# Cross-attention block: the Q, K, V and output products by seven blocks with sums in PSUM, softmax weights left undivided, and a new order on all engines

## The chip, the core and the metric

The kernel runs on one core of one Trainium2 chip. TensorE (PE) multiplies and writes only to PSUM; VectorE (DVE) and ScalarE (ACT) read and write PSUM and SBUF; GpSimd (POOL) works in SBUF; SyncE (SP) issues the transfers. The metric is the device time of one launch in microseconds (us). The median of the three runs is 1484.5 us (1484.43 to 1484.63).

## What is computed

There are 128 sequences of 128 tokens with 256 features, and a context of the same shape. All arithmetic is in fp32. Cut to what matters (16 heads of 16 features, `mask` is 0):

```python
q = (x @ Wq + bq) split into heads; k = (ctx @ Wk + bk); v = (ctx @ Wv + bv)
scores = q k^T / sqrt(16);  allowed = j < i;  scores = where(allowed, scores, -1e30)
attn = softmax(scores);  attn[:, :, 0, :] = 0
y = (attn v, heads joined) @ Wo + bo
x1 = layer_norm(x + y, ln1_g, ln1_b)
out = layer_norm(x1 + relu(x1 @ W1 + b1) @ W2 + b2, ln2_g, ln2_b)
```

W1 widens 256 to 1024 features and W2 brings them back.

## The kernel before

Two sequences make a pair, and one step handles one pair p: there are 64. The steps are a software pipeline. Step p computes the scores and the exponentials of pair p, the queries and keys of pair p+1, the weighted sum (`weigh`) and the output product of pair p-2, the W1 product of pair p-3 and the W2 product of pair p-4, and stores pair p-5. Pairs 0 to 6 fill the pipeline with code of their own, steps 7 to 62 are alike (`step`), step 63 and a written-out tail drain it. The order of the instructions on every engine is the order in which the functions are called: nothing reorders them, and an engine that waits holds up all that stands behind on it.

All of PSUM is one tile `banks` of eight banks of 512 columns. Scores of the high half of the rows take banks 0 to 3, of the low half banks 4 to 7, and the products take the same banks in turn.

**Products.** Q, K, V and the output product are each one block product of 256 x 256 weights with 256 columns: four matmuls of 128 x 128 weights by 256 columns (`project`, line 270; `values`, line 325; `attention_out`, line 573). In the trace every fp32 matmul is two records. The W1 and W2 products are already done by seven blocks (Strassen's scheme in Winograd's form): seven products of half blocks in place of eight, with sums of halves on the input side (`combine_normed`, `combine_hidden` on GpSimd) and sums of the products on the output side (`Hidden.u2` to `add5`, `sum_of_seven` on VectorE).

**Softmax.** ScalarE takes the exponential of each of the 32 head halves of a step, with the row sum beside it (`exponential_by_head`, line 839). VectorE takes reciprocals (`inverse`), GpSimd multiplies the weights by them in place (`divide`, line 485, three instructions a step), VectorE transposes 32 x 32 blocks into `tb` (`turn`, line 497), and 16 transfers a step move the blocks across partitions into `pT` (`bring`, line 512), from which `weigh` reads. The tiles `sm`, `tb` and `pT` share four buffers of one pool (`wide`).

**Norms.** Each of the two layer norms has its own statistics on VectorE and its own two scale factors on GpSimd (`deviation`, `shift`). ScalarE applies both (lines 625 and 662). The normed rows are transposed through DRAM (`turn_x1`): four transfers out, one back (lines 246 and 251).

**Transfers.** SP's queue holds in a step, in this order: 4 loads of x or of the context (line 92), in every second step one of the token rows (line 99), 4 plus 1 for the normed rows, the store (line 679), and the 16 of `bring`.

Of the kernel before, what the change touches and what calls it, by code (L numbers as in the profile page):

```python
# [10 lines left out]
ALU = mybir.AluOpType  # L11
# [8 lines left out]
def tile_cross_attention_block(  # L20
# [99 lines left out]
    def row(v, name):  # L120
        t = const.tile([P, v.shape[1]], F32, tag=name, name=name)
        nc.sync.dma_start(t, v.to_broadcast([P, v.shape[1]]))
        return t
# [11 lines left out]
    power = const.tile([P, 2, 1], F32, tag="power", name="power")  # L135
# [8 lines left out]
    table = const.tile([P, 2, 1], F32, tag="table", name="table")  # L144
# [3 lines left out]
    bo_r = row(bo, "bo_r")  # L148
# [7 lines left out]
    be1_r = row(ln1_b, "be1_r")  # L156
    b2_r = row(b2, "b2_r")
# [102 lines left out]
    def add_bo(p):  # L260
        st = states[p]
        st["xb"] = proj.tile([P, 2, D], F32, tag="xb", name=f"xb_{p}")
        nc.gpsimd.tensor_tensor(
            st["xb"], tokens_of[p // 2][:, p % 2 * 2 : p % 2 * 2 + 2], bov_r[:, None, :].to_broadcast([P, 2, D]), ALU.add
        )
# [92 lines left out]
    def wide(name):  # L358
        return soft.tile([P, NS * (H + HH) * 32], F32, tag="wide", name=name, bufs=4)

    def room(p, hi):

        st = states[p]
        if "sm" not in st:
            st["sm"] = wide(f"sm_{p}")
# [111 lines left out]
    def inverse(p, hi):  # L477
        st = states[p]
        rs = st["rs", hi] = small.tile([P, H], F32, tag=f"rs{hi}", name=f"rs{hi}_{p}")
        nc.vector.reciprocal(rs, st["su", hi])  # L480

    def divide(p, hi, part):
        st = states[p]
        sm = st["sm", hi]
        nc.gpsimd.tensor_tensor(  # L485
            sm[:, part, :], sm[:, part, :],
            st["rs", hi][:, part, None].to_broadcast([P, part.stop - part.start, sm.shape[2]]),
            ALU.mult,
        )
# [74 lines left out]
    def context(p):  # L564
        pc = states[p].pop("pc").rearrange("p (u i) -> p u i", i=P)
        nc.scalar.copy(cxT.rearrange("p m s i -> p (m s) i")[:, :, 1:], pc[:, :, 1:])  # L566
# [14 lines left out]
    def stats(p, t, i):  # L581
        st = states[p]
        mv = st["mv", i] = small.tile([P, 2, 2], F32, tag=f"mv{i}", name=f"mv{i}_{p}")
# [5 lines left out]
    def deviation(p, i):  # L589
# [3 lines left out]
        nc.gpsimd.tensor_scalar(ve, st["mv", i][:, :, 1:2], LN_EPS, None, ALU.add)  # L593
        nc.gpsimd.tensor_tensor(sd, ve, power, ALU.pow)

# [62 lines left out]
    def norm2(p):  # L658
        st = states[p]
        t2, sd, nb = st["t2"], st["sd", 2], st["nb", 2]  # L660
        for s in range(2):
            nc.scalar.activation(
                t2[:, s], t2[:, s], AF.Identity, bias=nb[:, s], scale=sd[:, s]
            )
# [74 lines left out]
    def turn_x1(p, queue=nc.sync, last=None, between=None):  # L739
        st = states[p]  # L740
        tb = ffn.tile([P, NS, 4 * 32], F32, tag="tbx", name=f"tbx_{p}")
# [25 lines left out]
    def hidden(p, fs, between=None, banks=(2, 3, 4, 0)):  # L767
        st = states[p]
        if fs[0] == 0:
            st["hT"] = ffn.tile([P, FC, TP], F32, tag="hT", name=f"hT_{p}", bufs=1)  # L770
# [60 lines left out]
    def exponential_by_head(p, hi, heads, summed=False):  # L831

        st = states[p]
        if summed and ("su", hi) not in st:
            st["su", hi] = small.tile([P, H], F32, tag=f"su{hi}", name=f"sa{hi}_{p}")
        sm, nmx = st["sm", hi], st["nmx", hi]
        for h in heads:
            src = st["sps", 1][h // 4][:, h % 4 * P : h % 4 * P + P] if hi else sm[:, h, :]
            nc.scalar.activation(sm[:, h, :], src, AF.Exp, bias=nmx[:, h : h + 1], scale=1.0, **(  # L839
                {"accum_out": st["su", hi][:, h : h + 1]} if summed else {}  # L840
            ))

    wt = const.tile([P, 4, FC // 2, P], F32, tag="wt", name="wt")
# [113 lines left out]
    class Hidden:  # L957
# [3 lines left out]
        def __init__(self, p, **where):  # L961
# [5 lines left out]
            else:  # L967
                self.hT = ffn.tile([P, FC, TP], F32, tag="hT", name=f"hT_{p}", bufs=1)
# [57 lines left out]
        def plain(self, fs, at):  # L1026
            ps = at_bank(at, f"ph_{self.p}_{fs[0]}")
            for i, f in enumerate(fs):
                self.plains[f] = ps[:, i * TP : (i + 1) * TP]
                for k in range(KC):  # L1030
# [4 lines left out]
                    )  # L1035

# [161 lines left out]
    def load_ahead(p):  # L1198
        if p % 2 == 0 and p + 4 < NP:
            load([p + 4, p + 5], "x")  # L1200
        if p % 2 == 1:
            if p + 3 < NP:
                load([p + 3, p + 4], "c")
            if 3 < p < NP - 1:
                load_tokens((p + 1) // 2)
# [106 lines left out]
    def fifth():  # L1312
# [34 lines left out]
        bring(p, nc.sync, LATE_FIRST)  # L1347
# [5 lines left out]
    def fall_in(p):  # L1353

        weigh(p - 2)
        context(p - 2)
        scores_both(p)
# [8 lines left out]
        exponential_by_head(p, 1, ONES)  # L1366
        mask_high(p, 2, 2)
        exponential_by_head(p, 1, TWOS)
# [3 lines left out]
        exponential_by_head(p, 0, ONES)  # L1372
        attention_out(p - 2)
        attention_sum(p - 2)
# [399 lines left out]
```

## Time and profile before

| | |
|---|---|
| median of three runs | 1484.5 us |
| span of the profiled execution | 1482.7 us |
| PE busy | 1475.0 us, 99% |
| DVE busy | 1386.3 us, 93% |
| ACT busy | 1324.1 us, 89% |
| POOL busy | 1376.5 us, 93% |
| transfers | 204.63 MB, mean 138 GB/s |

The page gives no time of the profiled execution beside its span; its span is 1.8 us below the median of the runs. Weighted sums of one step to the next start 22.63 us apart in each of the 56 steps 7 to 62, so these steps are 1267.6 us of the span; about 138 us lie ahead of them and 77 us behind. Matmuls are pipelined, so a busy PE tells only that there was always one in flight; how long a product holds PE is read from the starts of the product behind it.

### The profile page before, as it was taken

Reading aid. Unit: us, or ns where it says so; the run is one execution under the profiler, and the core shown is the slowest. Engines: PE = TensorE matmul, PEld = TensorE weight load, DVE = VectorE, ACT = ScalarE, POOL = GpSimd, SP = SyncE. Lnnn points to the kernel's source line nnn. Section 1 sums busy time; section 2 is a strip of 40 time slices with the busy share of each in tenths; the row PEclk is TensorE's granted clock in tenths of the full one; section 3 lists DMA queues with packets and bytes.
Section 4 is the critical chain, followed back from the end, with each engine's and each line's share of the span. In section 5 each row is a group of like instructions: output and inputs, shape, how many; then the busy total and the mean of one; then the engine's idle time right before and its main releaser. Section 6 shows DMA issues by size and latency. Waiting matters only on the chain.

```text
span 1482.7 us, 53916 instructions
## 1 busy us (share of the span) xinstructions
PE 1475.0 (99%) x19367; PEld 1378.1 (93%) x19367; DVE 1386.3 (93%) x2444; ACT 1324.1 (89%) x5272; POOL 1376.5 (93%) x1530
## 2 busy tenths in 40 slices
PE   9999999999999999999999999999999999999998
PEld 7788999999999999999999999999999999999998
DVE  7999999999999999999999999999999999999977
ACT  6668999999999999999999999999999999999963
POOL 6979999999999999999999999999999999999987
PEclk9999999999999999999999999999999999999999
DMA  8366666555655566665556556566655666555451
GB/s 201 79 133 150 148 150 141 127 146 138 154 144 133 138 146 138 149 144 130 144 132 156 146 128 143 144 137 150 145 132 141 136 153 148 128 141 131 109 137 51
DMA packets 415317, 204.63 MB, mean 138 GB/s; under 512 B 282448, under 2 KB 383056, under 8 KB 415056
## 3 DMA queue, kind: packets, MB, share of 16 engines
q1 hardware_dynamic: 412768, 199.34, 57.5%
q8 instruction: 160, 2.62, 0.8%
q10 hardware_dynamic: 2288, 1.85, 0.5%
q14 instruction: 101, 0.83, 0.2%
HBM read 70.26 MB, written 33.29 MB: 70 GB/s over the span
## 4 chain that ended last, share of the span: by engine, by line
PE 96%; DVE 2%; POOL 1%; ACT 0%; issue 0%; DMA 0%; POOLq 0%; DVEq 0%
PE banks L878 25%; PE banks L990 25%; PE banks L270 15%; PE banks L573 7%; PE banks L325 7%; PE banks L410 6%; PE banks L554 4%; PE banks L544 2%; PE banks L778 2%; PE banks L1042 0%; PE banks L797 0%; DVE su L468 0%; POOL sm L446 0%; PE banks L527 0%; POOL sm L470 0%
## 5 line engine op out<-in xcount | busy, mean ns | idle before, releaser
L839 ACT ACTIVATE sm<-banks,nmx 128x128 f32<-128x128 f32 x944 | 329.8, 377 | 16.3 <-DVE nmx L823 8.7
L485 POOL TENSOR_TENSOR sm<-sm,rs 128x1024 f32<-128x1024 f32 x171 | 322.6, 1901 | 0.0
L839 ACT ACTIVATE sm<-sm,nmx 128x64 f32<-128x64 f32 x944 | 312.5, 368 | 0.0
L497 DVE STREAM_TRANSPOSE tb<-sm 128x1024 f32<-128x1024 f32 x186 | 229.8, 1237 | 17.1 <-DMA pT<-tb 6.9
L1021 ACT ACTIVATE hT<-hT,b1e_c 128x256 f32<-128x256 f32 x464 | 198.1, 497 | 34.7 <-DVE hT L1009 21.0
L839 ACT ACTIVATION_READ_ACCUMULATOR sm<-sm,nmx 128x1 f32 x912 | 201.6, 221 | 0.0
L839 ACT ACTIVATION_READ_ACCUMULATOR sm<-banks,nmx 128x1 f32 x912 | 197.3, 216 | 0.0
L990 PE MATMUL banks<-xS,w1t 128*128 128x128 f32 x1392 | 174.4, 275 | 0.0
L878 PE MATMUL banks<-wt,hS 128*128 128x128 f32 x1440 | 170.7, 275 | 0.0
L878 PEld LDWEIGHTS banks<-wt,hS 128*128 128x128 f32 x1440 | 165.6, 192 | 0.1
L990 PEld LDWEIGHTS banks<-xS,w1t 128*128 128x128 f32 x1392 | 164.8, 192 | 0.0
L823 DVE TENSOR_REDUCE nmx<-banks 128x4 f32<-128x512 f32 x177 | 153.9, 869 | 6.0
L270 PE MATMUL banks<-xT,wq 128*128 128x256 f32 x504 | 125.4, 392 | 0.0
L315 ACT ACTIVATE kT<-banks,bkh,half 128x256 f32<-128x256 f32 x252 | 122.5, 590 | 2.8 <-PE banks L270 2.8
L990 PE MATMUL banks<-x1T,w 128*128 128x128 f32 x944 | 124.6, 275 | 0.2 <-DMA x1T<-x1t 0.2
L573 PE MATMUL banks<-wo,cxT 128*128 128x256 f32 x512 | 121.2, 379 | 0.0
L325 PE MATMUL banks<-wv,cT 128*128 128x256 f32 x512 | 121.0, 379 | 0.0
L270 PE MATMUL banks<-cT,wk 128*128 128x256 f32 x504 | 119.4, 380 | 0.1
L878 PEld LDWEIGHTS banks<-w,hT 128*128 128x128 f32 x944 | 114.7, 192 | 3.1
L990 PEld LDWEIGHTS banks<-x1T,w 128*128 128x128 f32 x944 | 114.9, 192 | 0.4 <-issue 0.3
L878 PE MATMUL banks<-w,hT 128*128 128x128 f32 x944 | 115.2, 275 | 0.0
L573 PEld LDWEIGHTS banks<-wo,cxT 128*128 128x128 f32 x512 | 97.0, 190 | 13.5 <-ACT cxT L566 0.3
(191 smaller groups left out, 3954.1 us busy)
## 6 DMA issues: line engine op xcount, KB each, us to landing
pT<-tb SPq DMA_DIRECT2D x976, 96.0 KB, 2.2
x1t<-tbx SPq DMA_DIRECT2D x252, 64.0 KB, 2.4
x1T<-x1t SPq DMA_DIRECT2D x63, 256.0 KB, 3.0
out_dram<-t SPq DMA_DIRECT2D x63, 256.0 KB, 3.1
xb<-in_x_dram SPq DMA_DIRECT2D x124, 128.0 KB, 3.7
cb<-in_ctx_dram SPq DMA_DIRECT2D x124, 128.0 KB, 4.2
x<-in_x_dram SPq DMA_DIRECT2D x31, 512.0 KB, 5.3
w<-in_L_xattn_W_dram SPq DMA_DIRECT2D x2, 1024.0 KB, 8.3
```

The source lines that it names most:

```text
L270: nc.tensor.matmul(ps[:, m * TP : (m + 1) * TP], w[:, k, m * P : (m + 1) * P], src[:, k, :], start=(k == 0), stop=(k == KC - 1),)
L315: nc.scalar.activation(st["kT"][:, m, e, :], pk[:, m * TP : (m + 1) * TP], AF.Identity, bias=bkh[:, m, e : e + 1], scale=half[:, e : e + 1],)
L325: nc.tensor.matmul(pv[:, s * D : (s + 1) * D], st["cT"][:, k, s * P : (s + 1) * P], wv[:, k, :], start=(k == 0), stop=(k == KC - 1),)
L410: nc.tensor.matmul(st["sps", hi][r][s * HP : (s + 1) * HP, m * 2 * n : (m + 1) * 2 * n].rearrange("p (e j) -> p e j", e=2), st["qT"][strip ...
L485: nc.gpsimd.tensor_tensor(sm[:, part, :], sm[:, part, :], st["rs", hi][:, part, None].to_broadcast([P, part.stop - part.start, sm.shape[2] ...
L497: nc.vector.transpose(st["tb"][:, :, at : at + 256].rearrange("p j (n a) -> p n j a", a=32), st["sm", hi].rearrange("p h j -> p (h j)")[:, ...
L573: nc.tensor.matmul(po[:, s * D : (s + 1) * D], cxT[:, k, s, :], wo[:, k, :], start=(k == 0), stop=(k == KC - 1),)
L823: nc.vector.tensor_reduce(st["nmx", 1][:, 4 * first : 4 * (first + n)], ps, AX.X, ALU.max, negate=True,)
L839: nc.scalar.activation(sm[:, h, :], src, AF.Exp, bias=nmx[:, h : h + 1], scale=1.0, **({"accum_out": st["su", hi][:, h : h + 1]} if summed ...
L878: nc.tensor.matmul(out, left(k), right(k), start=(k == 0), stop=(k == FC // 2 - 1))
L990: nc.tensor.matmul(ps[:, i * P : (i + 1) * P].rearrange("p (n a) -> p n a", a=32), left(i), right, start=True, stop=True,)
L1021: nc.scalar.activation(self.hT[:, f], self.plains.get(f, self.hT[:, f]), AF.Relu, bias=b1e_c[:, f : f + 1], scale=1.0,)
```

## The change

1. Q, K, V and the output product go by seven blocks too: seven matmuls of 128 x 128 by 128 columns in place of four by 256 columns. GpSimd forms the four sums of halves of each operand (`xc` of x, `cc` of the context for both K and V, `oc` of the attention context); the combined weights are formed once.
2. The sums of the products are made inside PSUM where the scheme allows it: a product block of class `Seven` is one bank with three regions a, b and f. Products 1, 6, 7 and 4 add onto a one after the other, 5 and 3 onto f, 2 goes to b. Between two of them ScalarE or VectorE takes the partial sum out of a, so PE must come back after that. W1 (`First`, three banks) and W2 (`Second`) now work in this way as well.
3. The exponentials stay undivided. All 32 row sums of a step go into one tile, VectorE takes the reciprocals and transposes them, SP writes them to DRAM (4 transfers) and reads them back broadcast (2 transfers), and `context` multiplies the attention context by them on VectorE in place of a ScalarE copy.
4. The two norms of a step share their statistics tiles and scale factors (`scales_of`); the second norm is applied on GpSimd (`norm2_on_pool`). `xb` is gone: the bias is added into the token tile in place. K is written once and spread to its two masked halves from SBUF (`spread`). The read back of the normed rows is issued a step later than the writes.
5. `sm`, `tb` and `pT` have one buffer each.
6. A step is a list of some 150 names, and each engine takes its own in the list's order. Names with -1 are run for the pair before. Pairs 7 to 62 use it.

```diff
@@ room, wide @@
-        return soft.tile([P, NS * (H + HH) * 32], F32, tag="wide", name=name, bufs=4)
+        return soft.tile([P, NS * (H + HH) * 32], F32, tag=name[:2], name=name, bufs=1)
@@ inverse and divide @@
-    def divide(p, hi, part):
-        st = states[p]
-        sm = st["sm", hi]
-        nc.gpsimd.tensor_tensor(
...
+    def inverse(p):
...
+        nc.vector.reciprocal(rs, st.pop("su"))
+        nc.vector.transpose(rt, rs)
+
+    def send_inverse(p):
...
+        for b in range(NS):
+            nc.sync.dma_start(mid[:, b], rt[32 * b : 32 * b + 32])
+
+    def fetch_inverse(p):
...
+        for m in range(KC):
+            nc.sync.dma_start(
+                inv[:, m].rearrange("p l s q -> p (l s q)"),
+                mid[m][:, None, :].to_broadcast([HH, DK, TP]),
+            )
@@ context @@
+            for l in range(2):
+                at = slice(l * HP + 1 - l, l * HP + HP)
+                nc.vector.tensor_tensor(
+                    cxT[:, :, :, at], pc[:, :, :, at], inv[:, :, l, :, 1 - l :], ALU.mult
+                )
@@ class Seven @@
+            for n in which:
+                out = self.of({2: 1, 5: 2, 3: 2}.get(n, 0))
...
+                for k in range(self.depth):
+                    nc.tensor.matmul(
...
+                        start=(n == 1 and k == 0), stop=(k == self.depth - 1),
...
+    class Queries(Seven):
...
+        def keep(self):
+            self.put(0, 0, self.a)
+            self.put(1, 1, self.f)
...
+        def keep2(self):
+            self.put(1, 0, self.a)
...
+        def add(self):
+            nc.vector.scalar_tensor_tensor(
+                self.q[:, 1, P:], self.a, QSCALE, self.q[:, 1, P:], ALU.mult, ALU.add
+            )
...
+        def rest(self):
+            self.put(0, 1, self.a)
@@ class Keys @@
+        def spread(self):
+            for e in range(2):
+                nc.scalar.activation(
+                    self.kT[:, :, e, :], self.k, AF.Identity, bias=0.0, scale=half[:, e : e + 1]
+                )
@@ the order of a step @@
+        weigh re2-1 inverse-1 res0-1 vr-1 tokc-1 re3-1 re0-1 hf-1 context scores res1-1 br3
...
+        load-1 hk ob w6 oa el3 xc3-1 stats2 xs0 kk q2 tokx xs1 el4 o4 cc3 sendi-1 w3 qk2 or
```

The first place is SP's queue. `inv` are the reciprocals in DRAM, `invb` their broadcast copy, `x1t` the normed rows in DRAM, `x1T` what is read back. Before, from one step's `pT` to the next:

```order
L512 DMA pT_12894<-tb_12765 32x768 x16
L92 DMA cb_13009<-in_ctx_dram 32x32x32 x4
L99 DMA x_13014<-in_x_dram 128x4x256
L246 DMA x1t_13222<-tbx_13219 32x4x128 x4
L251 DMA x1T_13221<-x1t_13222 128x4x128
L679 DMA out_dram<-t_32_12817 128x2x256
```

Now, from one step's first `pT` to its store (the token rows, `x`, come in every second step):

```order
L524 DMA pT_13454<-tb_13259 32x768 x4
L1918 DMA x1T_13476<-x1t_13328 128x4x128
L524 DMA pT_13454<-tb_13259 32x768 x12
L92 DMA xb_13570<-in_x_dram 32x32x32 x4
L490 DMA inv_13601<-rt_13405 32x32 x4
L498 DMA invb_13670<-inv_13601 128x1x256 x2
L99 DMA x_13686<-in_x_dram 128x4x256
L1913 DMA x1t_13701<-tbx_13688 32x4x128 x4
L730 DMA out_dram<-t_31_12748 128x2x256
```

Six transfers came in. The read back of `x1t` moved behind the next step's first four `pT`, and the read back of `inv` stands right behind its four writes.

The second place is PE behind the scores. Before, the four products of a step stand there in one piece (`wq`, `wo`, `wk`, `wv` are the weights, `w_139` is W2):

```order
L410 MATMUL banks<-kT_7739,qT_7719 64x128 x8
L270 MATMUL banks<-xT_7763,wq 128x256 x4
L573 MATMUL banks<-wo,cxT 128x256 x4
L270 MATMUL banks<-cT_7765,wk 128x256 x4
L325 MATMUL banks<-wv,cT_7410 128x256 x4
```

Now the blocks of V, of the output product, of Q and of W2 stand between each other (`wvt`, `wot`, `wqt`, `wt` are combined weights; `cc`, `oc`, `xc`, `hS` the combined halves):

```order
L409 MATMUL banks<-kT_7987,qT_7928 64x128 x8
L1146 MATMUL banks<-wv,cT_7832 128x128 x2
L1146 MATMUL banks<-wvt,cc_7968 128x128
L1146 MATMUL banks<-wo,cxT 128x128 x2
L1146 MATMUL banks<-wot,oc_8255 128x128
L1146 MATMUL banks<-w_138,hT 128x128 x4
L1146 MATMUL banks<-wvt,cc_7968 128x128
L1146 MATMUL banks<-wv,cc_7968 128x128
L1146 MATMUL banks<-xT_8015,wq 128x128 x2
```

PE no longer finishes a product before it starts the next: each product is cut into four parts, with other products between them.

The third place is ScalarE at the end of the exponentials. Before, the 32 exponentials (`sm<-`) are one piece, and the copies of Q, K, the hidden layer and V follow:

```order
L839 ACTIVATE sm_6556,sa_19_6614<-banks,nmx_19_6558 128x128 x16
L839 ACTIVATE sm_6556,sa_19_6635<-sm_6556,nmx_19_6557 128x64 x16
L296 ACTIVATE qT_6652<-banks,bqs_c 128x256 x2
L315 ACTIVATE kT_6672<-banks,bkh,half 128x256 x4
L999 COPY hT_6781<-banks 128x4x128
```

Now, up to the last block of Q (`kr` is K before it is spread, `x_32` the first norm):

```order
L891 ACTIVATE sm_12303,su_12384<-sm_12303,nmx_34_12304 128x64 x4
L668 ACTIVATE x_32_12552<-t_32_12363,nb_12525,sd_12524 128x256 x2
L1371 COPY hT<-banks 128x4x128
L891 ACTIVATE sm_12303,su_12384<-sm_12303,nmx_34_12304 128x64 x2
L1212 ACTIVATE kr_12450<-banks,bk_c 128x128
L891 ACTIVATE sm_12303,su_12384<-sm_12303,nmx_34_12304 128x64 x2
L1235 ACTIVATE kT_12451<-kr_12450,half 128x2x256 x2
L1174 ACTIVATE qT_12392<-banks,bqs_c 128x128
```

The exponentials are cut into groups of two to six heads, with the copies of partial sums between the groups.

More of the change, by code (lines that the diff above doesn't have):

```diff
@@ new lines, in residual1_one, with turn_x1_blocks @@
+    def residual1_one(p, n):
+        st = states[p]
+        if n == 0:
+            st["x1b"] = ffn.tile([P, 2, D], F32, tag="x1b", name=f"x1b_{p}", bufs=3)
+        nc.gpsimd.tensor_tensor(
+            st["x1b"], st["x1b"] if n else st["x1"],
+            (be1b_r if n else g1_r)[:, None, :].to_broadcast([P, 2, D]), ALU.add if n else ALU.mult,
+        )
+    def turn_x1_blocks(p):
+        st = states[p]
+        tb = st["tbx"] = ffn.tile([P, NS, 4 * 32], F32, tag="tbx", name=f"tbx_{p}", bufs=1)
+        nc.vector.transpose(
+            tb.rearrange("p j (u a) -> p u j a", a=32),
+            st["x1"].rearrange("p s (k j a) -> p (s k) j a", k=KC, a=32),
+        )
@@ L1560, in tile_cross_attention_block @@
     sixth(6)
-    for p in range(7, NP):
+    late = max(int((key + "-0").split("-")[1]) for key in ORDER)
+    for p in range(FIRST, NP - 1 + late):
         step(p)
+    last_step(NP - 1)
     VECTOR_ALONE = (nc.vector, nc.vector)
```

662 lines of the change are left out of this document (529 added, 133 removed).

## The prediction

> **What bounds the kernel now.** I read the page first, then a table of stretches, each one step long, then the timelines of the engines in one such step.
>
> The page, engine by engine, and the chain that ended last:
>
> ```profile
> span 1482.7 us, 53916 instructions
> PE 1475.0 (99%) x19367; PEld 1378.1 (93%) x19367; DVE 1386.3 (93%) x2444; ACT 1324.1 (89%) x5272; POOL 1376.5 (93%) x1530
> PE 96%; DVE 2%; POOL 1%; ACT 0%; issue 0%; DMA 0%; POOLq 0%; DVEq 0%
> ```
>
> One step, busy time of PE, weight loads, DVE, ACT, POOL, then the clock and the transfers:
>
> ```profile
> 313.13:335.76 22.63, 22.63 (x306) 21.36 (x306) 21.36 (x39) 21.34 (x90) 21.43 (x25) 1.00 0.58 129
> ```
>
> A step takes 22.63 us, PE never idles in it at clock 1.00, and the three other engines are at 94 to 95%. PE sets the pace, but whoever speeds up PE alone by 5% meets three other engines. There are 56 such steps, so 0.1 us a step is 5.6 us of the whole.
>
> PE's timeline in one step, from the Q product on (start, length, what):
>
> ```profile
> 344.97 1.99 PE L270 MATMUL banks<-xT,wq 128*128 128x256 f32 x8
> 346.80 1.89 PE L573 MATMUL banks<-wo,cxT 128*128 128x256 f32 x8
> 348.53 1.89 PE L270 MATMUL banks<-cT,wk 128*128 128x256 f32 x8
> 350.25 1.89 PE L325 MATMUL banks<-wv,cT 128*128 128x256 f32 x8
> 351.98 1.95 PE L878 MATMUL banks<-w,hT 128*128 128x128 f32 x16
> 353.77 1.06 PE L878 MATMUL banks<-wt,hT 128*128 128x128 f32 x8
> ```
>
> Starts tell the cost. The four products hold PE from 344.97 to 351.98, 7.01 us. Sixteen records of 128 columns take 1.79 us (351.98 to 353.77), so one takes 0.112.
>
> **PE after.** Each of the four products becomes seven matmuls, 14 records of 0.112: 1.57 us, 6.26 for all four. Everything else on PE keeps its count. The step falls by 0.75 to 21.88 us, if nobody keeps PE waiting.
>
> **ScalarE after.** Its timeline in the same step:
>
> ```profile
> 335.22 1.94 ACT L315 ACTIVATE kT<-banks,bkh,half 128x256 f32<-128x256 f32 x4
> 337.02 0.61 ACT L999 COPY hT<-banks 128x512 f32<-128x512 f32 x1
> 337.49 0.68 ACT L340 COPY vz<-banks 128x256 f32<-128x256 f32 x2
> 339.84 1.08 ACT L662 ACTIVATE t<-t,nb,sd 128x256 f32<-128x256 f32 x2
> 341.29 1.71 ACT L1021 ACTIVATE hT<-hT,b1e_c 128x256 f32<-128x256 f32 x4 [0.37 <-DVE hT L1009]
> 343.56 0.58 ACT L566 COPY cxT<-banks 128x508 f32<-128x508 f32 x1 [0.56 <-PE banks L554]
> 346.17 0.37 ACT L839 ACTIVATE sm<-banks,nmx 128x128 f32<-128x128 f32 x1
> 346.43 0.19 ACT L839 ACTIVATION_READ_ACCUMULATOR sm<-banks,nmx 128x1 f32 x1
> 357.13 0.85 ACT L296 ACTIVATE qT<-banks,bqs_c 128x256 f32<-128x256 f32 x2
> ```
>
> An activation of 128 columns holds ScalarE for 0.26 us (346.17 to 346.43); the two of Q now take about 0.72. Q becomes four of 128 columns, 1.04: plus 0.3. K costs 1.80 now (335.22 to 337.02); it becomes four of 128 columns, 1.04, and two spreads of 512, which I put at 0.65 each (the 512-column copy holds 0.47, plus what K's own 0.45 a piece shows of its pointer operands): plus 0.55. V's two copies become four: plus 0.3. The hidden copy becomes three: plus 0.95. The second norm and the context copy leave: about 1.0 and 0.45 less. The first half of the relus now reads PSUM: about 0.2 less. The net is 0.45 more. ScalarE is 21.34 busy with its ends counted, some 20.9 from start to start; after, 21.4, bounds 21.0 to 22.2.
>
> **VectorE after.** The prices by size, and the tail's rows for 128 columns:
>
> ```profile
> L919 DVE TENSOR_TENSOR t<-t,banks 128x256 f32<-128x256 f32 x120 | 50.6, 421 | 7.3 <-PE banks L878 3.3
> L1005 DVE TENSOR_TENSOR hT<-hT,banks 128x512 f32<-128x512 f32 x58 | 39.9, 688 | 7.0
> L1016 DVE TENSOR_TENSOR hT<-hT,banks 128x1024 f32<-128x1024 f32 x58 | 68.6, 1184 | 0.3 <-PE banks L990 0.2
> 1476.37 0.28 DVE L1706 TENSOR_TENSOR t_last<-banks,x1b 128x128 f32<-128x128 f32 x1
> ```
>
> Out go the sum of the output product (512 columns), five sums of W2 (512, twice 384, twice 256), six of the hidden layer (five of 512, one of 1024) and a reciprocal, together about 8.1 us. In come eleven adds of 128 columns (3.1), eight of 256, the two context products among them (3.4), three of 512 (2.1), the small transpose and the finer masks (0.5): 9.1. That is 1.0 more in durations; about 0.05 of each overlaps its neighbour (the step's 39 durations add up to some 23.2, busy is 21.4), so eleven more instructions give 0.5 back. VectorE comes to 21.8, bounds 21.2 to 22.4.
>
> **GpSimd after.** Its groups:
>
> ```profile
> L485 POOL TENSOR_TENSOR sm<-sm,rs 128x1024 f32<-128x1024 f32 x171 | 322.6, 1901 | 0.0
> L953 POOL TENSOR_TENSOR xS<-x1T 128x128 f32<-128x128 f32 x58 | 26.6, 458 | 0.0
> L594 POOL TENSOR_TENSOR sd<-ve,power 128x2 f32<-128x2 f32 x127 | 90.4, 712 | 10.6
> L1712 POOL TENSOR_TENSOR sd_last<-sd_last,power 128x1 f32<-128x1 f32 x2 | 1.3, 666 | 2.4 <-DVE sd_last L1711 2.4
> L593 POOL TENSOR_SCALAR ve<-mv 128x2 f32<-128x2 f32 x127 | 29.0, 228 | 15.2 <-DVE mv L587 4.7
> L1196 POOL TENSOR_TENSOR be1b_r<-be_r,b_r 128x256 f32<-128x256 f32 x1 | 0.7, 731 | 0.0
> ```
>
> Three divisions go: 5.7. Two sets of scale factors become one of four columns; the power costs 0.05 a column by the rows of one and two, so about 0.8, and the set about 1.3 less. Twelve sums of 128 columns come, 5.4. The second norm, two scalings of 256 columns, has no row: between 0.23 (two columns) and 0.73 (two inputs of 256 columns) each; I take 0.6, nearer to the row of its size. Sum: 0.4 less. Now 21.43 busy, 22.3 from start to start; after about 21.8 to 22.0, bounds 21.1 to 22.4. The Trainium skill, GPSIMD Engine Reference, section 3.1, puts a good loop at about 1.8 cycles an element where two inputs need 2.5. By that a scaling would be about 0.6, an estimate from that page, and GpSimd 21.9; no run here shows it.
>
> **SP's queue after.** SP computes nothing, but issuing takes its time, and a wait there holds up every later transfer. One step, and the waits of the queue (line waited for: total us, times, longest):
>
> ```profile
> 335.28 3.00 SPq L92 DMA_DIRECT2D cb<-in_ctx_dram  x4
> 338.32 1.98 SPq L99 DMA_DIRECT2D x<-in_x_dram  x1
> 340.71 1.84 SPq L246 DMA_DIRECT2D x1t<-tbx  x4
> 345.37 0.38 SPq L251 DMA_DIRECT2D x1T<-x1t  x1
> 345.85 0.45 SPq L679 DMA_DIRECT2D out_dram<-t  x1
> 346.38 10.99 SPq L512 DMA_DIRECT2D pT<-tb  x16
> SPq L251 <- DMA x1t<-tbx: 149.3, 109, 3.3
> ```
>
> Issuing takes 18.6 us in this step and 16.7 in one without token rows: 17.65 on average. On top SP stands from 342.55 to 345.37, 2.8 us, for the write to DRAM to land; over the 63 pairs 2.4 each. The change moves that read a step later, so the wait goes. It adds the same pattern anew: four small writes, with the read right behind them. The writes cost 1.2 (0.30 each, the shortest of `x1t`) to 1.84, I take 1.6; the two reads 0.38 to 0.45 each, 0.85; the landing 1.7 (the shortest `x1t`) to 2.8, I take 2.0, since fewer bytes go. Sum: 22.1, bounds 21.3 to 23.2. What used to hide it was 2 us of slack; the new step has less than none.
>
> **A deadline that is new.** `tb` had spare buffers and now has one. VectorE may write the next `tb` only when all 16 `pT` have landed:
>
> ```profile
> DVE tb L497 <- DMA pT<-tb: 6.9, 26, 1.4
> pT<-tb SPq DMA_DIRECT2D x976, 96.0 KB, 2.2
> ```
>
> The 16 can start only when `weigh` has read the single `pT`, about 1.5 us into the step. With 11.0 of issue, 0.4 of the read between them and 2.2 to land, the last is there at 15.1. VectorE reaches its `turn` by the sums above at about 13.9 to 14.5. It waits up to 1 us, and what stands behind on VectorE, about 9 us of work and at its end the context and the masks of the next step, comes late by as much. ScalarE has about 0.4 us to absorb that.
>
> **The sum.** PE 21.88, ScalarE 21.4, VectorE 21.8, GpSimd 21.9, SP 22.1; the largest is SP, and the deadline on `tb` pulls at the same figure. I add 0.15 for hand-overs, which were none before but are now four for each of six products, and take 22.25: 0.38 less in each of 56 steps, 21.3 us. Head and tail: the head loses six GpSimd divisions or their like and gains 24 small sums, the tail loses three and gains one trip through DRAM (about 5 us by the 2.4 and 3.0 us to land of `x1t` and `x1T`), so 0 to plus 5; I take plus 1. The span becomes 1482.7 - 21.3 + 1 = 1462.4, and the median, 1.8 above, 1464.
>
> **The rivals.**
>
> PE stays the bound (0.20): the handoffs fit, the landing is short, pT's issues come nearer to 0.6 each. Then 0.75 times 56: 42 off, 1443. For it speaks that PE lost nothing before with three engines at 95%.
>
> An engine's own work becomes the bound (0.10): VectorE or GpSimd at their upper 22.4 give 13 off, 1472.
>
> SP's queue makes it slower (0.22). Mechanism: SP waits for the four writes of the reciprocals as long as it waits for `x1t` today, with the upper issue costs: 17.65 + 1.84 + 0.9 + 2.8 = 23.2. It decides from 22.63 on, that is from 2.2 us of landing with these issue costs. Then 0.57 times 56 more: 1516. For it: the writes stand right behind four loads, as `x1t` stood behind the token rows when it took 2.8. Against it: they are far smaller.
>
> No change (0.04): SP at 22.6.
>
> The seven blocks save nothing (0.04). TensorE loads weights for every matmul, 56 loads in place of 32 for the four products, and the weight loads:
>
> ```profile
> L878 PEld LDWEIGHTS banks<-wt,hS 128*128 128x128 f32 x1440 | 165.6, 192 | 0.1
> L325 PEld LDWEIGHTS banks<-wv,cT 128*128 128x128 f32 x512 | 97.1, 190 | 13.2
> ```
>
> If a load that follows a wait is not hidden, 24 more at 0.19 are 4.6 us and the step grows by up to 3.9; already 0.75 undoes the gain. At half of that, 1.2 net, the time is 1552. The rows speak against it: in the existing seven blocks a load has 0.115 of busy time and the matmul behind it comes at 0.112, waits included. The Trainium skill, TensorE: Matmul & The Clock Gate, section LDWEIGHTS, gives 128 columns / 1.2, 107 ns, and Perfetto Trace Analysis, section Identifying the Most-Contended Engine, judges PE by its load share. By these the new blocks are bound by their loads; the trace's 0.112 agrees, and the sum already holds it.
>
> **How the numbers follow.** My forecast has 0.40. Faster: 0.40 + 0.20 + 0.10 = 0.70. Within 0.2%, about what a measurement of this kernel can tell: 0.04. Slower: 0.22 + 0.04 = 0.26. The range reaches from PE's bound, 1441, into the SP case as far as a step of 22.97, 19 us more: 1503. What lies beyond is most of the loads' case and half of SP's.
>
> **What would show it.** Starts of the weighted sums 22.25 apart; PE busy near 98% with idle time in front of the scores or `weigh`; SP's wait for `inv` near 2 us a step; VectorE waiting in `turn` for `pT`; records of 128 columns still 0.112 apart. The prediction is wrong if the step is below 21.9 or above 22.6, or if SP stands idle for over 2 us a step.

## The result, and the profile after

| | before | after |
|---|---|---|
| median of the runs | 1484.5 us | 1591.3 us (1584.8 to 1599.9) |
| ratio, 95% interval | | 1.072, 1.069 to 1.076 |
| span of the profiled execution | 1482.7 us | 1597.8 us |
| mean step, 7 to 62 | 22.63 us, all alike | 24.58 us, between 22.8 and 32.0 |

The change makes the kernel 7.2% slower; 1464 was forecast, with a range up to 1503. Of the 115 us more in the span, 56 steps with 1.95 more each make 109; the end after the last of them takes 4.0 more and the start 1.9. The longest step is the first in the new order (32.0). The profiled execution took 1599.9 us, the most of the six, so its steps stand some 0.15 us above those of the median.

First the busy time of the engines and the chain that ended last, by engine, from the page of the changed kernel.

```profile
PE 1508.3 (94%) x20711; PEld 1423.7 (89%) x20711; DVE 1328.2 (83%) x3114; ACT 1337.8 (84%) x5613; POOL 1398.5 (88%) x1933
PE 33%; SPq 29%; POOL 11%; DMA 9%; DVE 8%; issue 8%; ACT 2%; DVEq 0%; POOLq 0%; ACTq 0%
```

TensorE was busy 99% of the span and is at 94%; no engine is full. SP's queue, which computes nothing, has 29% of the chain. One step of that queue (start, duration, line, transfer, count):

```profile
707.40 3.34 SPq L524 DMA_DIRECT2D pT<-tb  x4
710.84 0.53 SPq L1918 DMA_DIRECT2D x1T<-x1t  x1
711.41 8.99 SPq L524 DMA_DIRECT2D pT<-tb  x12
720.45 2.86 SPq L92 DMA_DIRECT2D cb<-in_ctx_dram  x4
723.40 3.61 SPq L490 DMA_DIRECT2D inv<-rt  x4
728.17 1.31 SPq L498 DMA_DIRECT2D invb<-inv  x2
729.58 1.85 SPq L1913 DMA_DIRECT2D x1t<-tbx  x4
731.49 0.44 SPq L730 DMA_DIRECT2D out_dram<-t  x1
732.03 1.32 SPq L524 DMA_DIRECT2D pT<-tb  x1
```

From 707.40 to 732.03 SP issues or waits without a pause: 24.6 us. Its one long gap is from 727.01 to 728.17, where the reads of the inverses stand behind the landing of the four writes. With 23.5 us of issuing this is one of the long steps. Over all 56, with every pause of over 0.15 us between two issues counted as a wait, issuing takes 21.7 us a step (17.6 before), the pause ahead of the reads 1.7, and waits for engines and other transfers 1.2. The waits (line waited for: total us, times, longest) and two groups of GpSimd:

```profile
SPq L498 <- DMA inv<-rt: 85.7, 71, 2.9
DVE tb L509 <- DMA pT<-tb: 41.2, 26, 6.2
PE banks L1146 <- DVE t L1290: 30.0, 26, 5.2
PE banks L409 <- issue: 28.9, 19, 3.1
L713 POOL TENSOR_SCALAR t<-t,mv,sd 128x256 f32<-128x256 f32 x112 | 136.9, 1229 | 0.0
L1884 POOL TENSOR_TENSOR sd<-ve,power 128x4 f32<-128x4 f32 x56 | 58.1, 1038 | 0.0
```

Four causes could be read from these: SP's wait, the single `tb` (VectorE waits for `pT`, TensorE for the sums behind that), GpSimd, whose norm costs 1.23 us a half, and standstills of TensorE in the scores with no releaser. Each has 0.5 to 1.5 us a step, so the profile alone does not say which one sets it.

### The profile page after: what moved, and what is told of

Same layout as the page of the kernel before. It is cut to its first block, busy times and chain, and to the rows that moved or that the text cites. A ratio compares the mean times of both kernels' runs of the same rounds, so it can differ in the third digit from the quotient of the medians.

```text
span 1597.8 us, 56966 instructions
## 1 busy us (share of the span) xinstructions
PE 1508.3 (94%) x20711; PEld 1423.7 (89%) x20711; DVE 1328.2 (83%) x3114; ACT 1337.8 (84%) x5613; POOL 1398.5 (88%) x1933
## 3 DMA queue, kind: packets, MB, share of 16 engines
q8 instruction: 166, 2.72, 0.8%
## 4 chain that ended last, share of the span: by engine, by line
PE 33%; SPq 29%; POOL 11%; DMA 9%; DVE 8%; issue 8%; ACT 2%; DVEq 0%; POOLq 0%; ACTq 0%
SPq L524 24%; PE banks L1146 14%; PE banks L1355 10%; DMA pT<-tb 4%; DMA x<-in_x_dram 3%; PE banks L409 2%; PE banks L566 2%; DVE tb L509 2%; POOL t L713 2%; POOL x1b L1895 2%; SPq L1918 1%; PE banks L556 1%; DVE t L1290 1%; SPq L92 1%; POOL t L727 1%
## 5 line engine op out<-in xcount | busy, mean ns | idle before, releaser
L891 ACT ACTIVATE sm<-sm,nmx 128x64 f32<-128x64 f32 x944 | 320.5, 356 | 0.0
L409 PE MATMUL banks<-kT,qT 32*64 32x256 f32 (+1 forms) x3840 | 124.0, 336 | 34.1 <-issue 28.9
L1850 DVE TENSOR_REDUCE nmx<-banks 128x4 f32<-128x512 f32 x224 | 143.2, 681 | 0.0
L1839 POOL TENSOR_TENSOR hS<-hT 128x512 f32<-128x512 f32 x112 | 140.3, 1274 | 0.0
L409 PEld LDWEIGHTS banks<-kT,qT 32*64 32x64 f32 x3840 | 89.2, 132 | 57.1 <-issue 33.2
L713 POOL TENSOR_SCALAR t<-t,mv,sd 128x256 f32<-128x256 f32 x112 | 136.9, 1229 | 0.0
L1384 ACT ACTIVATE hT<-hT,b1e_c 128x256 f32<-128x256 f32 x224 | 95.6, 497 | 29.4 <-DVE hT L1380 29.4
L1290 DVE TENSOR_TENSOR t<-banks,t 128x256 f32<-128x256 f32 x224 | 69.0, 348 | 46.5 <-PE banks L1146 46.5
L1844 DVE TENSOR_TENSOR banks<-banks,neg 128x256 f32<-128x256 f32 x224 | 94.7, 423 | 4.5 <-PE banks L409 4.5
L1390 ACT ACTIVATE hT<-banks,b1e_c 128x256 f32<-128x256 f32 x224 | 94.5, 481 | 0.5 <-PE banks L1355 0.5
```

Source lines behind the costliest of these rows:

```text
L409: nc.tensor.matmul(st["sps", hi][r][s * HP : (s + 1) * HP, m * 2 * n : (m + 1) * 2 * n].rearrange("p (e j) -> p e j", e=2), st["qT"][strip ...
L713: nc.gpsimd.tensor_scalar(t2[:, s], t2[:, s], mv[:, s, 0:1], sd[:, s], ALU.subtract, ALU.mult)
L1384: nc.scalar.activation(self.hT[:, f, at], self.hT[:, f, at] if src is None else src, AF.Relu, bias=b1e_c[:, f : f + 1], scale=1.0,)
L1390: nc.scalar.activation(self.hT[:, 2 * i].rearrange("p (s t) -> p s t", s=2), banks[:, self.at : self.at + 2, i * P : (i + 1) * P], AF.Relu ...
L1839: nc.gpsimd.tensor_tensor(c[:, n], left, right, how)
L1844: nc.vector.tensor_tensor(ps[:, :, HP:], ps[:, :, HP:], neg[:, 1, None, :].to_broadcast([P, 4, HP]), ALU.add)
```

## The experiments

All are edits of the changed kernel unless another is named. Times are medians; before was 1484 us in every comparison. "Step" is the mean from start to start of `weigh` in the profiled execution, and the median step stands beside it where the two differ in meaning.

**SP and GpSimd: four kernels.** The second norm back on ScalarE; the inverses read later; both; the norm and no trip at all (that kernel multiplies the context by a constant, so it leaves the division out).

```
-        "norm2": lambda p: norm2_on_pool(p - 5),
+        "norm2": lambda p: norm2(p - 5),                      # e1, e3, e4
-  ... norm1 fetchi ka ...   h3 finish1 qr store-1 re1
+  ... norm1 ka ...          h3 finish1 qr fetchi store-1 re1  # e2, e3
-        "sendi": lambda p: send_inverse(p),
+        "sendi": lambda p: states[p].pop("rt"),               # e4
```

> The changed kernel with the second norm back on ScalarE, as before the change: two scalings of 1.23 us leave GpSimd (23.4 us of own work a step become 20.9), two of some 0.5 us come to ScalarE. If GpSimd's own work sets the step of 24.58, the step falls to the next bound, 22.3 to 23.0: 1465 to 1505 us. If SP's queue with the single tb and pT sets it, GpSimd only gets idle time: 1580 to 1600 us. If TensorE's standstills in the scores (28.9 us in all, no releaser shown) are a cost of their own, they stay in every kernel.

> The changed kernel with the read of the inverses moved in the order from ahead of the token rows to ahead of the store, after the writes of x1: same transfers, but SP no longer stands 1.6 us a step for the four small writes to land. If SP's queue sets the step: 24.58 less 1.6, 23.0, times 56: about 1500 us. If GpSimd's own work of 23.4 sets it: 1530 at the least (24.58 to 23.4 only if that idle time came from SP), or no change, 1580 to 1600.

> Both edits: second norm on ScalarE and the inverses read late. If SP alone sets the step: as the late read alone, about 1500. If GpSimd alone: as the norm alone. If both bind by turns, each alone brings little and the two together bring the step to 22.3 to 22.6: 1465 to 1485 us.

> Second norm on ScalarE, and the inverses' trip through DRAM left out in steps 7 to 62 (reciprocals are still computed; the context is multiplied by a constant, so the division is not done): 6 transfers and the wait for their landing go from SP, some 5 us a step. If SP's queue sets the step, TensorE's 21.9 to 22.1 becomes the bound: 1445 to 1460 us. If the step stays above 23 here, neither SP nor GpSimd's norm is the cause, and it is in the order of the work or TensorE's standstills: above 1500 us.

Measured: 1598.4, 1583.2, 1597.0 and 1547.9 us (steps 24.54, 24.32, 24.49, 23.75). GpSimd with 2.5 us less a step gains nothing, so alone it does not set the step here. The late read misses its forecast of 1500: SP's wait for the inverses is gone (1.4 us in all), but SP now stands for VectorE's transposed rows ahead of the writes of `x1t`, and the answer comes late.

```profile
SPq L1913 <- DVE tbx L1903: 96.2, 51, 5.7
DVE cxT L582 <- DMA invb<-inv: 74.9, 41, 3.8
PE banks L409 <- DVE cxT L582: 48.9, 44, 3.2
```

In that kernel the context waits for `invb`, and the scores for the context: part of the wait went from SP to TensorE. Without the trip 50 us go against the same norm on its own. That speaks for the trip, by SP's load or by its answer; but 1445 to 1460 was forecast for SP as the only bound, and the step stays at 23.75, so SP is not all.

**TensorE's code blocks and the sums behind `tb`: four kernels.** 23 times after step 7 starts, TensorE stood still over 0.2 us before an instruction that waits for nothing, 31.3 us in all, mostly in the scores; before, never. One such place, as a table of stretches (us, busy time and count of each engine, granted clock, DMA share, GB/s), and the instruction queue in the page:

```profile
316.00:318.00 2.00, 2.00 (x134) 1.82 (x124) 1.31 (x3) 1.52 (x5) 1.92 (x2) 1.00 0.82 210
318.00:320.00 2.00, 0.35 (x15) 0.00 (x0) 1.38 (x5) 1.75 (x5) 1.15 (x3) 1.00 1.07 336
320.00:322.00 2.00, 0.86 (x26) 0.59 (x26) 0.36 (x2) 0.00 (x0) 2.00 (x4) 1.00 0.31 103
322.00:324.00 2.00, 2.00 (x12) 2.00 (x13) 1.89 (x4) 0.96 (x5) 2.00 (x4) 0.62 0.45 110
324.00:326.00 2.00, 2.00 (x12) 2.00 (x11) 2.00 (x5) 0.94 (x6) 1.23 (x2) 0.53 0.70 219
326.00:328.00 2.00, 2.00 (x20) 2.00 (x20) 1.64 (x3) 1.52 (x8) 0.00 (x0) 1.00 0.66 160
q8 instruction: 166, 2.72, 0.8%
```

TensorE stands from 318.4 to 321.1, at first while the transfers fill every DMA engine. Soon after it runs 3.4 us at half its clock, which the rows of two us average to 0.62 and 0.53:

```profile
322.47:325.88 3.41, 3.41 (x19) 3.41 (x18) 3.41 (x8) 1.90 (x10) 2.76 (x3) 0.50 0.63 179
```

Counted through the trace (matmuls, weight loads, semaphore and empty instructions), all 23 standstills fall on the same number modulo 256, and at each of them TensorE goes on 1.2 to 1.6 us after a packet of the instruction queue has landed. The row `q8 instruction` has 2.72 MB in 166 packets, 16 KB each; TensorE's 42,670 instructions in 166 blocks are 257 a block. Before has 640 instructions a step, two and a half blocks, so the block's edge falls on the same two places for ever. 22 of the 640 are empty instructions in the second layer, and the new order has none:

```profile
L219 PEldq NOP  x1700: 13/13/13, 1.1 to 1468.6; - x189
L221 PEldq NOP  x468: 13/13/13, 1.1 to 1583.8; - x156
```

The first row is before's, the second after's; the difference is 22 in each of 56 steps. After has 668 instructions a step, and the edge wanders through the dense stretch of `weigh` and scores.

```
-  ... means k2 turn1 eh1 ... wb xs2 wa addbo turn0 el1 k3 w4 norm1 fetchi ka xc0 kb ...
+  ... means k2 eh1 ... wb xs2 wa addbo el1 k3 w4 norm1 fetchi ka turn1 turn0 xc0 kb ...   # e5, e7
+        fill()    # behind each matmul: empty ones, 36 in step 7, then 100 a step           # e6, e7
-                empty(after // (FC // 2) + (after % (FC // 2) > k))                         # e8, in before
```

> The changed kernel with one move in VectorE's order: the transposes turn1 and turn0 into the single tb stand behind the second layer's two sums and the first sum of the keys, not ahead of them. Theory tb: TensorE's last product of the second layer waits for those sums, and they stand behind a turn that waits for all 16 pT to land (some 1.6 us in 26 steps), so the loop weigh, 16 issues, landing, turn, sums, TensorE's rest sets many steps: 0.6 to 1.0 us less a step, 1535 to 1560 us. Theory SP or GpSimd: unchanged, 1580 to 1600. Theory code blocks: unchanged too, the stalls in the scores stay at about 30 us.

> The changed kernel with 100 empty instructions a step on TensorE (36 in step 7), each beside a matmul of 128 columns, so that a step has 768 instructions in place of 668. Theory code blocks: TensorE's instructions come in blocks of 256 (the trace has 166 packets of 16 KB in an instruction queue, and every stall without a wait stands at the same number modulo 256). With 668 a step the block's edge wanders and falls badly into the dense stretch of weigh and scores in four steps of ten; with 768 it stands at one harmless place. Then the stalls (31 us) and the slow clock behind them go: 1535 to 1565 us, less if the tb loop fills the gap. All other theories: unchanged, 1585 to 1605, or a little slower for the added instructions.

> Both edits at once: sums ahead of the turns, and 768 instructions a step. If the two causes are apart from each other, their gains add: 1490 to 1520 us. If one hides behind the other, it comes to no more than the larger of the two alone.

> The kernel before without the 22 empty instructions a step that stand in its second layer, which the change drops too: 618 instructions a step in place of 640, which is two and a half blocks of 256. Theory code blocks: the edge wanders here as well and stalls of 1 to 2 us appear in the scores in some four steps of ten, with a slow clock behind them: 1505 to 1535 us. If the block's edge does not matter, 22 instructions fewer change nothing: 1483 to 1485 us.

Measured: 1617.6, 1616.4, 1613.1 and 1495.7 us. The last one shows the blocks: before without its 22 empty instructions is 0.7% slower (0.6 to 0.9; 11.8 us, less than the 20 or more forecast), with 8 standstills, 6.4 us, where there were none, all at the same number modulo 256 as in after. The rest of the loss is not taken apart.

```profile
PE banks L410 <- issue: 6.4, 8, 1.7
```

The padded kernel has no standstill left, and yet it is 25 us slower, against the forecast. SP's wait for the inverses rose from 85.7, and TensorE's for the context from 3.0:

```profile
SPq L498 <- DMA inv<-rt: 118.2, 76, 3.0
PE banks L409 <- DVE cxT L582: 26.0, 29, 3.1
```

TensorE's waits for the sums behind `tb` rose as well, from 30.0 to 42.0, and those for `x1T` from 6.3 to 16.7: together 45 us more where 31 went. So the standstills are real and lay beside longer waits. Why the landing takes longer there stays open. The moved transposes failed as an experiment: `kb`, the second sum of the keys, now stood behind both of them, and TensorE waited for it instead.

```profile
PE banks L1146 <- DVE kr L1228: 82.0, 56, 5.3
```

**SP's wait taken away without delaying its answer: four kernels.** The inverses are sent ahead of the block loads, so that the loads lie between the writes and the reads; the trip then in one write and one read; then the norm on ScalarE; then the padding.

```
-  ... k1 load-1 hk ... cc3 sendi-1 w3 ...
+  ... k1 sendi-1 load-1 hk ... cc3 w3 ...                          # e9 to e12
-        for b in range(NS):
-            nc.sync.dma_start(mid[:, b], rt[32 * b : 32 * b + 32])
+        nc.sync.dma_start(mid.rearrange("r b c -> b r c"), rt)     # e10 to e12
```

> The changed kernel with one move in SP's order alone: the four small writes of the inverses go ahead of the four block loads, so that the loads lie between the writes and the reads that wait for them. Nothing is done less, and the reads stand where they stood. The trace of the changed kernel shows SP issuing or waiting without a gap, 24.6 us a step, 1.6 to 3.0 of them in that wait. Theory SP: the wait goes, 1.5 us less a step, 1500 to 1515 us. Theory tb loop or GpSimd: under 0.3 us a step, 1575 to 1600.

> The same move, and the inverses' trip in one write and one read in place of four and two (the sums' columns are numbered so that one transfer can do it): four issues fewer, about 2.1 us of SP a step. Theory SP: SP at some 21.5 us a step is no bound any more; GpSimd's own work of 23.0 to 23.4 is the next: 1500 to 1520 us, little better than with the move alone. If GpSimd does not bind: 1465 to 1490.

> Move, one trip, and the second norm back on ScalarE (GpSimd 20.9 us a step, ScalarE 22.5). Theory SP first, GpSimd second: now the norm counts, where it was worth nothing alone: 30 to 40 us less than without it, 1465 to 1485 us. If GpSimd does not bind: equal to the kernel without this part.

> All of that and the 100 empty instructions a step on TensorE, which took every stall in the scores away but gained nothing while SP set the step. With SP and GpSimd off the path TensorE is near the bound, and stalls and slow clock (0.3 to 0.7 us a step) should now count: 15 to 35 us less than without them, 1440 to 1465 us, below the kernel before. If they still bring nothing, another loop sets the step.

Measured: 1547.7, 1545.2, 1551.6 and 1537.2 us; the ranges forecast for SP as the cause, 1500 to 1515 for the first, were too low. Still, one word moved in the order takes 44 us off. SP's wait falls to 4.1 us in all:

```profile
SPq L498 <- DMA inv<-rt: 4.1, 4, 1.9
SPq L524 <- PE banks L566: 59.0, 55, 1.7
```

SP now waits for `weigh` 55 times: it has time to spare. The step is 23.60, 0.98 less, where 1.5 was forecast. That the wait in SP's queue cost these 44 us is shown. Four transfers fewer bring nothing more, so SP's load is no bound after that. The forecast that the norm would count now was wrong: 6 us slower. The padding, worth nothing before, brings 14 us (five standstills, 3.5 us, are left, now in `weigh`). In the chain of the padded one SP's issuing of `pT` has 29%. One step of it (start, duration, what):

```profile
730.40 0.57 SPq L522
...
740.98 0.60 SPq L522
741.58 0.04 issue
741.62 2.19 DMA pT<-tb
...
744.23 0.10 DVE tb L507
744.32 1.07 issue
745.39 0.25 DVE vz L1271
745.65 0.54 DVE t L1297 x2
```

This is the deadline on `tb`: sixteen issues and the read between them, 11.2 us, landing, the transpose, the sums of the second layer, and TensorE's products behind those.

**The loop through the single `tb`: three kernels that moved it, two that cut it.** First both transposes behind the sums of the second layer and of the keys, on the kernel with early sends, on the padded one, and on that one with the norm on GpSimd.

```
-  ... means k2 turn1 eh1 ... wa addbo turn0 el1 k3 w4 norm1 fetchi ka xc0 kb h7 ...
+  ... means k2 eh1 ... wa addbo el1 k3 w4 norm1 fetchi ka xc0 kb turn1 turn0 h7 ...   # e13 to e15
```

> The kernel with the inverses sent early (1547.7 us), and the transposes turn1 and turn0 into the single tb moved behind both sums of the second layer and both sums of the keys, so that nothing TensorE waits for soon stands behind them (the earlier trial left the second sum of the keys behind them, and TensorE waited 1.5 us a step for that instead). Theory tb loop: weigh, 16 issues of 11.4 to 12 us, landing 2.2, turn 1.15, sums 0.8, TensorE's last 5.5 and weigh 1.8 make 23 to 23.5 us a step; with the turn and the sums taken out of the way TensorE no longer waits, 0.4 to 0.8 us less a step: 1500 to 1525 us. If GpSimd's own work (23.0 to 23.4) sets it now, under 0.2 a step: 1535 to 1550.

> The best so far (1537.2 us: sent early, one trip, norm on ScalarE, 768 instructions a step), with the same move of the two transposes. Theory tb loop: TensorE is left with its own 22.05 us and hand-overs of 0.2 to 0.5 a step: 1450 to 1485 us, at or below the kernel before. If it stays above 1520, the loop through tb is not what holds it.

> As that one, but the second norm stays on GpSimd as in the changed kernel. Theory GpSimd second: its 23.0 to 23.4 us a step now bind, 25 to 60 us more than with the norm on ScalarE: 1505 to 1530 us. If GpSimd's work is no bound even so: equal within 8 us.

Measured: 1583.6, 1559.7 and 1562.8 us, all slower than what they were built on. Two transposes on end, 2.4 us, now stood ahead of the sums of the queries and the hidden layer, for which TensorE waits in every step of the second of these kernels (22.8 and 39.3 us in all). This says nothing for or against the loop. So `tb` got its second buffer back, with no order changed; the room came from other tiles.

```
-        return soft.tile([P, NS * (H + HH) * 32], F32, tag=name[:2], name=name, bufs=1)
+        return soft.tile([P, NS * (H + HH) * 32], F32, tag=name[:2], name=name, bufs=2 if name[:2] in ('tb',) else 1)
     # qT, kT, t1, invb: bufs=1; x1b: bufs=2
```

> The kernel with the inverses sent early (1547.7 us), and two buffers for tb as before the change, paid for with single buffers for qT, kT, t1 and invb and two in place of three for x1b. The order of every engine is that of the kernel it is built on. Theory tb loop: VectorE's turn no longer waits for the 16 pT of the pair before to land, so the loop weigh, issues, landing, turn, sums, rest of TensorE is cut: 0.4 to 0.9 us less a step, 1497 to 1525 us; GpSimd's 23.0 or so is then the next bound. If the tb loop is no cause: 1540 to 1555, or slower where a single buffer costs something.

> The best so far (1537.2 us: sent early, one trip, norm on ScalarE, 768 instructions a step on TensorE) with two buffers for tb. With SP, GpSimd, code blocks and the tb loop all relieved TensorE's own 22.05 us a step is left, plus 0.2 to 0.6 for hand-overs: 1448 to 1475 us, faster than both kernels. If it stays at 1530 to 1540, the loop through tb is not what holds it and something else is.

Measured: 1537.6 us on the early sends (1547.7) and 1520.8 us on the best so far (1537.2). Both miss their forecasts, but the steps have become even: median 23.25 and 22.96. With the norm on GpSimd (36% of the whole chain) the part of the chain shown runs through GpSimd alone, from the means to the last sum for the output product:

```profile
927.44 0.23 POOL ve L1882
...
931.33 2.43 POOL t L713 x2
...
943.77 0.42 POOL oc L1826
944.19 0.04 issue
944.24 1.38 PE banks L1146 x10
```

and with the norm on ScalarE (17% of the whole chain) mostly through ScalarE, from the scores to the last copy that frees `weigh`'s bank:

```profile
725.04 1.50 ACT sm L889 x8
...
742.60 0.26 ACT qT L1181
742.87 0.04 issue
742.91 0.32 PE banks L554 x8
```

The kernel with early sends alone already had a median step of 23.29, so most of its steps were not held by `tb`: of the 7.5 us between the two profiled executions 7.2 lie in the first step (29.9 against 24.3) and ahead of it. That GpSimd's loop held them is read from the chain and not shown: with one `tb`, taking the norm off GpSimd gained nothing (1545.2 to 1551.6), and no kernel takes only that off with two. On the relieved kernel the buffer cut a loop of its own: the mean step falls by 0.28, of which 0.12 is the first step alone.

**A version built from all this.** The two halves of the norm go to VectorE and GpSimd, none to ScalarE, and the read of `x1T` goes ahead of the sixteen `pT`.

```
-        for s in range(2):
-            nc.gpsimd.tensor_scalar(
+        for s, engine in enumerate((nc.vector, nc.gpsimd)):
+            engine.tensor_scalar(
-  ... scores res1-1 br3 ...   xc1-1 readx-1 o1 ...   kb h7 norm2 qa ... loadx turnx el5
+  ... scores res1-1 readx-1 br3 ...   xc1-1 o1 ...   kb h7 qa ... loadx turnx norm2 el5
```

> The best so far (1520.75 us; two buffers for tb, one early trip for the inverses, 768 instructions a step), with two edits: the second norm's two scalings divided between VectorE (0.41 us, which has some 2.5 us idle a step) and GpSimd (1.23 us) in place of ScalarE, and the read of x1 ahead of the 16 pT in SP's queue. Theory: with tb's second buffer the steps have become even and show one engine each: 23.24 with both scalings on GpSimd, 22.95 with both on ScalarE. So the step should go to the next engine: ScalarE 22.0 to 22.4, GpSimd 21.7 to 22.2, TensorE 22.05 to 22.4; 0.5 to 0.9 us less a step, and the late x1 of some steps (0.2 us a step) with it: 1470 to 1492 us. If the step stays at 22.95 it was not ScalarE's work that set it.

Measured: 1485.4 us (1476.4 to 1492.9), ratio 1.000 (0.998 to 1.002): the changed kernel repaired is as fast as before, not faster. What each of the two edits brought is not separated. Its chain, and four steps of it as a stretch:

```profile
PE 81%; DMA 6%; SPq 4%; DVE 4%; ACT 3%; issue 1%; POOL 1%; DVEq 0%; POOLq 0%; ACTq 0%
910.89:999.36 88.47, 88.47 (x1314) 86.66 (x1313) 83.19 (x205) 85.45 (x373) 83.21 (x121) 1.00 0.68 153
```

Here TensorE is full and a step takes 22.12 us. 22 of 56 steps are like that; the others are up to 2.5 us longer, the mean 22.67, and the chain gives 3% to the landing of `invb`. What is left of the gain, 0.5 us a step, goes to those longer steps, and the end takes 2.8 us more than before.

## Why the prediction was wrong

**SP's queue, the term that failed.** The prediction put it at 22.1, bounds 21.3 to 23.2. By the count over 56 steps it is 23.4, 21.7 of issuing and 1.7 of waiting for the inverses. The landing was not undersized (2.0 was put). The issuing was, by 1.6: four writes of inverses take 2.3 on average for 1.6, two reads 1.3 for 0.85, the sixteen `pT` 11.4 for 11.0, and the gaps and other issues the rest. The 12.3 for the sixteen in the step shown is rare, 5 of 56 steps are over 12.2; with the early sends they take 11.4 on average too, so it is not the fuller queue that lengthens them. The other step that failed is the 0.15 for hand-overs: SP stands another 1.2 a step for engines and other transfers, and 23.4 and 1.2 make the 24.6. The rival "SP's queue makes it slower", with 0.22, had the mechanism: the writes stand right ahead of the read that waits for them. Its 23.2 a step is near SP's own 23.4; what it lacks is the 1.2. Worse, the forecast took the order of the transfers as given and did not ask whether SP had to stand there: the block loads, 2.9 us of issuing, stood on the wrong side of the wait.

**GpSimd's scaling.** The half norm was put at 0.6, between 0.23 and 0.73; it measured 1.23, outside the bounds. Neither row used was of its kind: the small one has two columns, the large one two inputs and no operand held per partition. The estimate from the Trainium skill, GPSIMD Engine Reference, section 3.1, was about 0.6 too, by that page's best case of about 1.8 cycles an element; the measurement decides, and this instruction took twice that. (For two inputs section 3.1 has 2.6, where the prediction wrote 2.5; nothing in the sum rests on it.) The power of four columns took 1.04 for 0.8. The 56 steps of the changed kernel as one stretch, for this and the next paragraph:

```profile
140.07:1516.85 1376.77, 1298.76 (x18369) 1242.58 (x18369) 1152.39 (x2800) 1203.77 (x5207) 1226.25 (x1734) 0.98 0.60 141
```

GpSimd is busy 21.9 us a step; from start to start, as the forecast counted, it takes 22.2, for 21.9. The doubled scaling shows in its durations, which add up to 23.0 us a step for 22.0 before, and not from start to start (22.2 before and after): neighbouring instructions overlap more than they did. Alone it did not set the step.

**What the sum could not see.** VectorE (20.6 for 21.8) and ScalarE (21.5 for 21.4) came out below or near the forecast, and TensorE, 21.88 forecast, reached 22.12 where nothing holds it. The sum took the largest engine and 0.15 for hand-overs. The floors that the runs laid bare (SP 24.6, then 23.25 with the norm on GpSimd, `tb`, and 22.96 with it on ScalarE) look like loops that pass from queue to engine and back, longer than any engine's own work: with two `tb` and the norm on GpSimd, GpSimd works 22.2 us a step and waits 1.2 for VectorE's statistics. "The deadline on `tb`" was named, at up to 1 us of wait; VectorE waits 26 times, 1.6 on average and 6.2 at most, and cutting the loop was worth 0.28 a step once SP was relieved. Of the 107 us lost, the wait in SP's queue is 44 by a single edit; the other 62 went with the later edits together, and how they divide among the loops is shown only in part.

**What was missed.** That the new order drops 22 empty instructions a step, each 13 ns and hidden, was not seen as a change. Taking them from the kernel before cost 11.8 us, and 100 a step put into the half repaired kernel brought 14. The seven blocks themselves did most of what the forecast said: records of 128 columns still start 0.112 apart (the median, before, after and in the last version), so loads are hidden, and TensorE saves 0.5 us a step for 0.75; where the rest went was not taken apart. The rival on the loads also took 0.75 off twice: half of 4.6 less 0.75 is 1.55 a step, 1571 and not 1552.

## What to carry to other kernels

Before costing a change by engine sums, walk each queue's order for a wait that stands between a transfer and its landing, and put other issues into that gap; one such word was worth 44 us here. When a tight kernel has single buffers, trace the loops (issue, landing, use, hand-back) and not only the engines' totals, and relieve several at once before judging one, since each edit alone shows only the largest. Instructions that seem to do nothing may hold the stream's length: count the instructions of a step before dropping them.

## What the hardware showed

TensorE's instructions arrive in blocks of 256 through a DMA queue of their own (166 packets of 16 KB for 42,670 instructions). In the changed kernel TensorE stood up to 3.1 us at a block's edge, mostly in the dense stretch, and work went on 1.2 to 1.6 us after a block had landed. Around the seven standstills of 1.6 us and more the DMA engines were 79 to 98% busy (from 1 us ahead to the end); around the sixteen shorter ones 22 to 85%, so full DMA engines go with the long ones and are not needed for a short one. Empty instructions on the weight-load side take 13 ns each and move the block's edge; whether a hundred a step cost time of their own, no run separates.

The standstill of 2.8 us was followed by 3.4 us at 0.50 of the clock, so it can cost more than its length. It does not always: one of 2.3 us, at 515.8, was followed by full clock, one of 1.6 us, at 954.6, by 3.4 us at half. The Trainium skill, TensorE: Matmul & The Clock Gate, section What's actually happening, states half clock after an idle window of about 3.4 us; the half agrees with this trace, but the pauses ahead of it were shorter.
